# Attention scores: three products of 308 columns, or one of 308 and two of 154

## The chip, the cores and the metric

The kernel runs on one core of a Trainium2 chip. The metric is the time on the device in microseconds (us), the median of the runs shown. The core's engines are TensorE (PE in the profile, its weight loads PEld), VectorE (DVE), ScalarE (ACT), GpSimd (POOL) and SyncE (SP), whose queue issues the DMAs here. Each works through its own queue in order and meets the others at semaphores.

## The reference, cut to what matters

The inputs are x, 32 batches of 512 rows by 640 columns, and a context of 32 batches of 77 rows by 1024. There are 20 heads of 32 columns.

```python
q = _heads(hidden_states @ to_q_w)
h_txt = _sdpa(q, _heads(ehs_txt @ to_k_w), _heads(ehs_txt @ to_v_w))
...
s = jnp.einsum('bhqd,bhkd->bhqk', q, k) * scale
p = jax.nn.softmax(s, axis=-1)
return jnp.einsum('bhqk,bhkd->bhqd', p, v)
...
out = out @ to_out_w + to_out_b
out = (out + residual) / RESCALE
```

The context has exactly 77 rows, so the three further groups of keys (object, others, image) are empty and add nothing. Each head's scores are 512 x 77 numbers, a sum over the head's 32 columns.

## The kernel before, in words

**High and low parts.** All matrix products are of float32r operands. To keep float32 precision each operand is split in two float32r tiles: `split` (L100) lets ScalarE copy the source, which rounds it (the high part, L101), and VectorE subtract that from the source (the low part, L102). A product is then three matmuls into one PSUM tile: high x high, high x low and low x high (`PAIRS`, L120).

**First phase.** Up to about 295 us the kernel turns the context into keys and values, in five groups of 512 or fewer context rows. The keys' high and low parts go out to `k_dram` (L176), the values' to `v_dram`. The weights of the queries and of the output are split as well. This phase's order is made by a scheduler.

**Slots.** Then come 160 slots, each a call of `slot(n)`: batch b = n // 5, chunk j = n % 5 of four heads. From here the order on each engine is as written (`manual_schedule`). A slot has four score tiles t of 128 rows. `scores` (L334) multiplies the 128 queries of the four heads (128 partitions, 32 for each head) with the key tile kb, which is block diagonal: head i's keys stand in partitions 32 i to 32 i + 31 and in columns 77 i to 77 i + 76, and all else is zero. So one matmul of 308 columns gives the scores of four heads. VectorE takes the maximum of each head (nm), `exps` (L353) lets ScalarE write the exponentials and their sums. Three PSUM buffers hold score tiles.

Around that, a slot n works on several n at once:

- `queries(n + 1)` (L316) makes the next chunk's queries in the PSUM tile pq, and `split_q` (L330) splits them into qt, of which there are two.
- `normalize(n - 1)` on GpSimd (L373) divides, and `transpose_p` (L377) transposes on VectorE to z and stores z to DRAM (pd). `load_p` (L393) brings pd back, with keys in the partitions (raw), for a chunk two slots back.
- `cast_p` (L400) and `rest_p` (L407) split raw into pp: ScalarE L404 and L410, VectorE L411, GpSimd L414. The slot begins with `cast_p` on ScalarE.
- `values` (L422) multiplies pp with vb into pa, `split_a` splits that into at.
- `piece` (L472) makes a part of an earlier batch's output, `finish` (L480) adds the residual and bias and stores it.
- The next batch's x is loaded at j = 4 (`load_x`), transposed on VectorE (`transpose_x`, L264) and split (`split_x`, L268) by ScalarE and GpSimd, at the places that `TRANSPOSE_X` and `SPLIT_X` name for each j: three lists, for the three places in a slot. The split x lies in eight buffers xt, five to a batch.
- `refill` (L512) is the slot's first step. At j = 0 and 2 it issues `load_keys` (L295), four DMAs for one of the two groups of chunks; at j = 1 and 3 it issues `load_values`. All go through SP's queue, in order, in front of raw, the residual and pd's stores of that slot.

In the first slots, up to n = 3, no values and no output are made, so TensorE has less to do there.

Of the kernel before, what the change touches and what calls it, by code (L numbers as in the profile page):

```python
# [8 lines left out]
F32 = mybir.dt.float32  # L9
FPR = mybir.dt.float32r  # L10
AF = mybir.ActivationFunctionType
ALU = mybir.AluOpType
# [11 lines left out]
P = 128  # L24
Q = 32
HEADS = 20
HD = 32
# [23 lines left out]
def kernel(  # L51
# [21 lines left out]

    nc = tc.nc
    B, S, C = x.shape
    CA = ehs.shape[2]
# [82 lines left out]
    def keys(g0, gn, j, k):  # L161
        if k == 0:
            pks[j] = psk.tile([P, G], F32, tag="ps", name="pk")
        for n, (a, c) in enumerate(PAIRS):
            nc.tensor.matmul(  # L165
                pks[j][:, :gn],
                wk_s[:, k, a, j * P : (j + 1) * P],
                cts[k][:, c, :gn],
                start=(k == 0 and n == 0),
                stop=(k == NK - 1 and n == 2),  # L170
            )
        if k == NK - 1:
            pk = pks.pop(j)
            ks = kvt.tile([P, 2, G], FPR, tag="ks", name="ks")
            split(ks[:, 0, :gn], ks[:, 1, :gn], pk[:, :gn])
            nc.sync.dma_start(  # L176
                k_dram[:, j, :, g0 : g0 + gn].bitcast(F32), ks[:, :, :gn].bitcast(F32)
            )

    values_of = {}  # L180

# [96 lines left out]

    kbs, vbs, pnb = [], [], []
    for g, (j0, nj) in enumerate(GROUPS):  # L280
        kb = main.tile([P, nj, 2, KCOLS], FPR, name=f"kb{g}")
        nc.gpsimd.memset(kb.bitcast(F32), 0.0)
        kbs.append(kb)
# [4 lines left out]
    qts = [main.tile([P, 2, S], FPR, name=f"qt{n}") for n in range(2)]  # L288
# [5 lines left out]

    def load_keys(b, g):  # L295
        j0, nj = GROUPS[g]
        for i in range(HPC):
            r = slice(i * HD, (i + 1) * HD)
            nc.sync.dma_start(
                kbs[g][r, :, :, i * NKEY : (i + 1) * NKEY].bitcast(F32),  # L300
                k_dram[r, j0 : j0 + nj, :, b * NKEY : (b + 1) * NKEY].bitcast(F32),
            )

    def load_values(b, g):
        j0, nj = GROUPS[g]
# [22 lines left out]
                )  # L328

    def split_q(n):  # L330
        qt = qts[n % 2]
        split(qt[:, 0, :], qt[:, 1, :], pqs.pop(n))

    def scores(n, t):  # L334
        b, j = divmod(n, NC_)
        g = GROUP_OF[j]
        qt, kb = qts[n % 2], kbs[g][:, j - GROUPS[g][0]]
        sc = ps.tile([P, S], F32, tag="sc", name="sc", bufs=3)
        for m, (a, c) in enumerate(PAIRS):
            nc.tensor.matmul(  # L340
                sc[:, :KCOLS],
                qt[:, a, t * P : (t + 1) * P],
                kb[:, c, :],
                start=(m == 0),
                stop=(m == 2),
            )
# [88 lines left out]

    def split_a(n):
        if n >= N - NC_ + 1:
            at = main.tile([P, 2, S], FPR, tag="xt", name="at", bufs=8)
# [72 lines left out]

    def refill(b, j):  # L512

        if j == 0 and b >= 1:
            load_keys(b, 1)
        elif j == 1 and b >= 1:
            load_values(b, 0)
        elif j == 2 and b + 1 < B:
            load_keys(b + 1, 0)
        elif j == 3 and b >= 1:  # L520
            load_values(b, 1)

    def slot(n, beside=None):
# [210 lines left out]
```

## Time and profile before

| | |
|---|---|
| median of 3 runs | 2027.37 us (2027.36 to 2029.03) |
| the profiled execution | 2028.15 us, its span 2026.0 us |
| granted TensorE clock, mean | 0.991 |
| TensorE busy | 1990.2 us of the span (98%) |
| ScalarE busy | 1397.0 us (69%) |
| VectorE busy | 1253.3 us (62%) |
| GpSimd busy | 1051.7 us (52%) |
| DMA, hardware queue | 530013 packets, 414.77 MB, 78.7% of 16 engines' span |
| score matmuls | 1920 of 308 columns, 640 tiles |
| one batch (five slots) in the steady part | 52.95 us |

How to read it: a span is the time from the first to the last instruction of one profiled execution; the run that holds it is a little longer. A group's line gives source line, engine, operation, output<-input, shapes, count, then the busy time in us, the mean of one in ns and the engine's idle time ahead of it with what ended it. A matmul's duration includes the way through the array and overlaps with the next, so what a matmul costs in a row of them is the distance from one start to the next. A bracket behind a line of the timeline is idle time ahead of it and what released it.

### The profile page before, as it was taken

What the parts mean: (1) busy time and instruction counts of PE and PEld (TensorE: products, weight loads), DVE (VectorE), ACT (ScalarE), POOL (GpSimd) and SP (SyncE); (2) the same over time, 40 slices, a digit from 0 to 9 for tenths busy, and PEclk for the clock granted to TensorE, in tenths of its full rate; (3) what the DMA queues carried; (4) which work ended last, traced back from release to release, by engine and by line L of the source; (5) the groups of instructions that cost most, each with busy time, mean ns of one, the idle gap of its engine ahead of it and who ended that gap; (6) DMA issues with size and microseconds to landing.
All of it is one profiled execution on the core that took longest, in us unless ns stands there. A gap on an engine that the chain in (4) does not pass through costs nothing.

```text
span 2026.0 us, 37077 instructions
## 1 busy us (share of the span) xinstructions
PE 1990.2 (98%) x11012; PEld 1802.7 (89%) x11012; DVE 1253.3 (62%) x1999; ACT 1397.0 (69%) x6057; POOL 1051.7 (52%) x615
## 2 busy tenths in 40 slices
PE   8899997999999999999999999999999999999998
PEld 7799986899999999999999999999999999999997
DVE  5443235566666666666666666666666666666663
ACT  3322127777778777777777777777778777787772
POOL 0000024666666666666656566666666666666654
PEclk9999998999999999999999999999999999999999
DMA  7963267988888888888888888888888887888865
GB/s 188 250 217 99 103 151 167 230 211 218 219 219 218 211 220 217 214 215 221 218 216 219 210 223 207 216 216 222 218 215 211 214 216 214 220 215 216 221 187 157
DMA packets 530212, 417.14 MB, mean 206 GB/s; under 512 B 144415, under 2 KB 433725, under 8 KB 530013
## 3 DMA queue, kind: packets, MB, share of 16 engines
q1 hardware_dynamic: 530013, 414.77, 78.7%
q8 instruction: 90, 1.47, 0.3%
q14 instruction: 109, 0.89, 0.1%
HBM read 239.30 MB, written 175.32 MB: 205 GB/s over the span
## 4 chain that ended last, share of the span: by engine, by line
PE 92%; DMA 3%; SPq 1%; ACT 1%; DVE 1%; issue 0%; POOL 0%; DVEq 0%; ACTq 0%; POOLq 0%
PE po L458 28%; PE pq L322 27%; PE pa L428 15%; PE sc L340 13%; PE pk L165 5%; PE pv L191 5%; DMA cs<-in_ctx_dram 1%; ACT pn L358 1%; DMA raw<-pd 0%; SPq L149 0%; SPq L111 0%; DVE z L380 0%; DMA xs<-in_x_dram 0%; DMA wraw<-in_L_xattn_to_out_w_dram 0%; SPq L387 0%
## 5 line engine op out<-in xcount | busy, mean ns | idle before, releaser
L358 ACT ACTIVATE pn<-sc,nm 128x77 f32<-128x77 f32 x2560 | 799.4, 329 | 105.1 <-DVE nm L348 101.4
L458 PE MATMUL po<-wo_s,at 128*128 128x320 f32 x3840 | 615.9, 310 | 5.2 <-DVE xr L486 5.2
L322 PE MATMUL pq<-xt,wq_s 128*128 128x512 f32 x2400 | 610.9, 395 | 0.0
L458 PEld LDWEIGHTS po<-wo_s,at 128*128 128x128 f32 x3840 | 576.5, 188 | 5.8 <-DVE xr L486 5.5
L414 POOL TENSOR_TENSOR pp<-raw,pp 64x512 fp32r<-64x512 f32 x160 | 283.2, 1770 | 512.5 <-ACT pp L410 510.0
L358 ACT ACTIVATION_READ_ACCUMULATOR pn<-sc,nm 128x1 f32 x2560 | 530.3, 207 | 0.0
L322 PEld LDWEIGHTS pq<-xt,wq_s 128*128 128x128 f32 x2400 | 437.3, 188 | 79.8
L348 DVE TENSOR_REDUCE nm<-sc 128x4 f32<-128x308 f32 x640 | 299.7, 469 | 297.0 <-PE sc L340 294.9
L373 POOL TENSOR_TENSOR pn<-pn,rs 128x1232 f32<-128x1232 f32 x160 | 364.1, 2276 | 33.1 <-DVE rs L368 20.9
L340 PE MATMUL sc<-kb,qt 128*128 128x308 f32 x1920 | 377.8, 306 | 2.4 <-ACT qt L101 1.7
L340 PEld LDWEIGHTS sc<-kb,qt 128*128 128x128 f32 x1920 | 325.4, 188 | 45.2 <-ACT qt L101 2.4
L428 PE MATMUL pa<-pp,vb 128*128 128x512 f32 x1280 | 331.5, 401 | 10.7 <-ACT pp L404 9.5
L380 DVE STREAM_TRANSPOSE z<-pn 128x1280 f32<-128x1280 f32 x160 | 241.8, 1511 | 78.8 <-POOL pn L373 29.4
L428 PEld LDWEIGHTS pa<-pp,vb 128*128 128x128 f32 x1280 | 246.0, 198 | 49.9 <-ACT pp L404 10.0
L274 POOL TENSOR_TENSOR xt<-xs,xt 128x512 fp32r<-128x512 f32 x157 | 202.6, 1294 | 149.0 <-ACT xt L273 145.6
L101 ACT CAST at<-pa 128x512 fp32r<-128x512 f32 x160 | 94.0, 588 | 256.8 <-PE pa L428 256.6
L411 DVE TENSOR_TENSOR pp<-raw,pp 128x1024 fp32r<-128x1024 f32 x160 | 196.1, 1226 | 50.6 <-ACT pp L404 50.3
L451 POOL TENSOR_TENSOR xr<-xr,bias 128x640 f32<-128x640 f32 x128 | 201.4, 1574 | 1.8 <-DMA xr<-in_x_dram 1.7
L404 ACT CAST pp<-raw 128x1024 fp32r<-128x1024 f32 x160 | 169.4, 1059 | 5.3 <-DMA raw<-pd 4.9
L165 PE MATMUL pk<-ct,wk_s 128*128 128x512 f32 (+1 forms) x600 | 137.8, 391 | 9.8 <-ACT ct L101 9.8
L191 PE MATMUL pv<-wv_s,ct 128*128 128x320 f32 (+1 forms) x960 | 143.6, 311 | 1.8 <-DVE vs L102 1.8
L191 PEld LDWEIGHTS pv<-wv_s,ct 128*128 128x128 f32 (+1 forms) x960 | 140.9, 186 | 4.0 <-DVE vs L102 2.1
(37 smaller groups left out, 1099.1 us busy)
## 6 DMA issues: line engine op xcount, KB each, us to landing
pd<-z SPq DMA_DIRECT2D x640, 160.0 KB, 3.8
raw<-pd SPq DMA_DIRECT2D x160, 512.0 KB, 4.2
xs<-in_x_dram SPq DMA_DIRECT2D x128, 320.0 KB, 7.5
xr<-in_x_dram SPq DMA_DIRECT2D x128, 320.0 KB, 4.7
out_dram<-xr SPq DMA_DIRECT2D x128, 320.0 KB, 3.5
raw<-pd SPq DMA_DIRECT2D x160, 128.0 KB, 4.4
v_dram<-vs SPq DMA_DIRECT2D x19, 640.0 KB, 3.7
k_dram<-ks SPq DMA_DIRECT2D x20, 512.0 KB, 3.3
```

Of the source, the lines that this page charges most:

```text
L165: nc.tensor.matmul(pks[j][:, :gn], wk_s[:, k, a, j * P : (j + 1) * P], cts[k][:, c, :gn], start=(k == 0 and n == 0), stop=(k == NK - 1 and ...
L191: nc.tensor.matmul(pv[:tn, :HALF], cts[k][:, a, t0 : t0 + tn], wv_s[:, k, c, h * HALF : (h + 1) * HALF], start=(k == 0 and n == 0), stop=( ...
L274: engine.tensor_tensor(parts[1], src, parts[0].bitcast(F32), ALU.subtract)
L322: nc.tensor.matmul(pqs[n], wq_s[:, k, a, j * P : (j + 1) * P], xts[b, k][:, c, :], start=(k == 0 and m == 0), stop=(k == NC_ - 1 and m == 2),)
L340: nc.tensor.matmul(sc[:, :KCOLS], qt[:, a, t * P : (t + 1) * P], kb[:, c, :], start=(m == 0), stop=(m == 2),)
L348: nc.vector.tensor_reduce(nm, sc[:, :KCOLS].rearrange("p (h k) -> p h k", k=NKEY), AX.X, ALU.max, negate=True)
L358: nc.scalar.activation(pnb[n % 2][:, at, :NKEY], sc[:, i * NKEY : (i + 1) * NKEY], AF.Exp, bias=nm[:, i : i + 1], accum_out=sms[n][:, at : ...
L373: nc.gpsimd.tensor_tensor(pf, pf, rs.unsqueeze(2).to_broadcast([P, NQ * HPC, NKEY]), ALU.mult)
L380: nc.vector.transpose(z.rearrange("p b t j -> p t b j"), pn.rearrange("p (t h) k -> p t (h k)", t=NQ).rearrange("p t (b i) -> p t b i", i=Q),)
L414: nc.gpsimd.tensor_tensor(pp[64:, 4, :], raw[:64, 2, :], pp[:64, 4, :].bitcast(F32), ALU.subtract)
L428: nc.tensor.matmul(pas[n], vb[:, t, :, a], pp[:, c, :], start=(m == 0), stop=(m == len(PASSES) - 1),)
L458: nc.tensor.matmul(pos[b, t, h][:, :HALF], ats[b * NC_ + j][:, a, t * P : (t + 1) * P], wos[0][:, j, c, h * HALF : (h + 1) * HALF], start= ...
```

## The change

The score tile's three products become one of 308 columns and two of 154.

- The first is as before: high queries of all four heads with high keys, block diagonal, 308 columns.
- The second makes the columns of heads 0 and 1. These two heads fill only 64 partitions. In the other 64 the new query tile holds a second copy of the same two heads: low queries in partitions 0 to 63, high queries in 64 to 127. The new key tile kc holds the high keys under the low queries, and the low keys under the high queries. So one matmul of 154 columns adds both low x high and high x low.
- The third does the same for heads 2 and 3, with halves exchanged.

To make them, `split_q` writes three query tiles and not two: ScalarE's high copy as before, then for each half one subtraction on VectorE (64 partitions) and one copy on ScalarE of 64 partitions from PSUM into the opposite half. The keys are stored in DRAM in the arrangement that kc needs, by four DMAs of 64 partitions for one before. `load_keys` issues two DMAs for each head, kb (high keys) and kc (both), eight for four before.

The tile qt grows by half, and xt has seven buffers for eight. The transposes and splits of the next x move: the splits are two at j = 2 and three at j = 3, where they were one, two and two at j = 1, 2 and 3. In the middle of the slot `finish` stands before the transposes and not behind. The keys of the second group and the values of batch 0 are loaded in the first slots and no longer ahead of them.

```diff
+            for w in range(2):
+                for half in range(2):
+                    nc.sync.dma_start(
+                        k_dram[half * 64 : half * 64 + 64, j, w, g0 : g0 + gn].bitcast(F32),
+                        ks[w * 64 : w * 64 + 64, int(half != w), :gn].bitcast(F32),
+                    )
...
-        xt = main.tile([P, 2, S], FPR, tag="xt", name="xt", bufs=8)
+        xt = main.tile([P, 2, S], FPR, tag="xt", name="xt", bufs=7)
...
+        kb = main.tile([P, nj, KCOLS], FPR, name=f"kb{g}")
+        kc = main.tile([P, nj, 2, KCOLS // 2], FPR, name=f"kc{g}")
...
     def load_keys(b, g):
         j0, nj = GROUPS[g]
+        kb, kc = kbs[g]
+        src = k_dram[:, j0 : j0 + nj, :, b * NKEY : (b + 1) * NKEY].bitcast(F32)
         for i in range(HPC):
-            r = slice(i * HD, (i + 1) * HD)
+            r, half = slice(i * HD, (i + 1) * HD), i % 2 * NKEY
             nc.sync.dma_start(
-                kbs[g][r, :, :, i * NKEY : (i + 1) * NKEY].bitcast(F32),
-                k_dram[r, j0 : j0 + nj, :, b * NKEY : (b + 1) * NKEY].bitcast(F32),
-            )
+                kb[r, :, i * NKEY : (i + 1) * NKEY].bitcast(F32), src[r, :, i // 2, :]
+            )
+            nc.sync.dma_start(kc[r, :, :, half : half + NKEY].bitcast(F32), src[r])
...
     def split_q(n):
-        qt = qts[n % 2]
-        split(qt[:, 0, :], qt[:, 1, :], pqs.pop(n))
+
+        qt, pq = qts[n % 2], pqs.pop(n)
+        nc.scalar.copy(qt[:, 0, :], pq)
+        lower, upper = slice(0, 64), slice(64, P)
+        for w, (r, other) in enumerate(((lower, upper), (upper, lower))):
+            nc.vector.tensor_tensor(
+                qt[r, 1 + w, :], pq[r], qt[r, 0, :].bitcast(F32), ALU.subtract
+            )
+            nc.scalar.copy(qt[other, 1 + w, :], pq[r])
...
+        for m, (cols, keys_) in enumerate(
+            (
+                (slice(0, KCOLS), kb[:, jg]),
+                (slice(0, half), kc[:, jg, 0]),
+                (slice(half, KCOLS), kc[:, jg, 1]),
+            )
+        ):
             nc.tensor.matmul(
-                sc[:, :KCOLS],
-                qt[:, a, t * P : (t + 1) * P],
-                kb[:, c, :],
+                sc[:, cols],
+                qt[:, m, t * P : (t + 1) * P],
+                keys_,
...
-    TRANSPOSE_X = {0: ((), (0,), (1,)), 1: ((2,), (3,), ())}
-    SPLIT_X = {1: ((), (0,)), 2: ((1,), (2,)), 3: ((3,), (4,))}
+    TRANSPOSE_X = {0: ((), (0,), ()), 1: ((1,), (2,), ()), 2: ((3,), (), ())}
+    SPLIT_X = {2: ((0,), (1,)), 3: ((2, 3), (4,))}
...
-        if j == 0 and b >= 1:
+        if j == 0:
             load_keys(b, 1)
-        elif j == 1 and b >= 1:
+        elif j == 1:
             load_values(b, 0)
...
+        finish()
         for i in turns[1]:
             transpose_x(b + 1, i)
-        finish()
...
         load_keys(0, 0)
-        load_keys(0, 1)
-        for g in range(2):
-            load_values(0, g)
```

More of the change, by code (lines that the diff above doesn't have):

```diff
@@ L175, in keys @@
             split(ks[:, 0, :gn], ks[:, 1, :gn], pk[:, :gn])
-            nc.sync.dma_start(
-                k_dram[:, j, :, g0 : g0 + gn].bitcast(F32), ks[:, :, :gn].bitcast(F32)
-            )
+            for w in range(2):
[4 more added lines that the diff above has]
+                    )
     values_of = {}
@@ L280 @@
     for g, (j0, nj) in enumerate(GROUPS):
-        kb = main.tile([P, nj, 2, KCOLS], FPR, name=f"kb{g}")
-        nc.gpsimd.memset(kb.bitcast(F32), 0.0)
-        kbs.append(kb)
+        kb = main.tile([P, nj, KCOLS], FPR, name=f"kb{g}")
+        kc = main.tile([P, nj, 2, KCOLS // 2], FPR, name=f"kc{g}")
+        for tile_ in (kb, kc):
+            nc.gpsimd.memset(tile_.bitcast(F32), 0.0)
+        kbs.append((kb, kc))
     for n in range(2):
@@ L287 @@
         pnb.append(pn)
-    qts = [main.tile([P, 2, S], FPR, name=f"qt{n}") for n in range(2)]
+    qts = [main.tile([P, 3, S], FPR, name=f"qt{n}") for n in range(2)]
     z = main.tile([P, NBLK, NQ, Q], F32, name="z")
@@ L336, in scores @@
         g = GROUP_OF[j]
-        qt, kb = qts[n % 2], kbs[g][:, j - GROUPS[g][0]]
+        qt, (kb, kc) = qts[n % 2], kbs[g]
+        jg = j - GROUPS[g][0]
         sc = ps.tile([P, S], F32, tag="sc", name="sc", bufs=3)
-        for m, (a, c) in enumerate(PAIRS):
+        half = KCOLS // 2
+        for m, (cols, keys_) in enumerate(
[5 more added lines that the diff above has]
+        ):
             nc.tensor.matmul(
-                sc[:, :KCOLS],
-                qt[:, a, t * P : (t + 1) * P],
-                kb[:, c, :],
+                sc[:, cols],
+                qt[:, m, t * P : (t + 1) * P],
+                keys_,
                 start=(m == 0),
@@ L437, in split_a @@
         if n >= N - NC_ + 1:
-            at = main.tile([P, 2, S], FPR, tag="xt", name="at", bufs=8)
+            at = main.tile([P, 2, S], FPR, tag="xt", name="at", bufs=7)
         else:
@@ L519, in refill @@
             load_keys(b + 1, 0)
-        elif j == 3 and b >= 1:
+        elif j == 3:
             load_values(b, 1)
```

## The prediction

> **What bounds the kernel now.** I read the page's busy times first, then PE's timeline over one slot (a slot is one of the 160 calls of `slot`, one group of four heads in one batch), then the groups and the waits.
>
> ```profile
> PE 1990.2 (98%) x11012; PEld 1802.7 (89%) x11012; DVE 1253.3 (62%) x1999; ACT 1397.0 (69%) x6057; POOL 1051.7 (52%) x615
> ```
>
> TensorE is busy 98% of the span; the next engine, ScalarE, 69%. A busy share may hide gaps, so the slot from 1001.66 (the third of a batch's five, j = 2) follows; columns are start, length with the pipeline's tail, line, count.
>
> ```profile
> 1001.66 0.59 PE L340 MATMUL sc<-kb,qt 128*128 128x308 f32 x3
> 1002.09 1.55 PE L322 MATMUL pq<-xt,wq_s 128*128 128x512 f32 x6
> 1003.48 0.60 PE L340 MATMUL sc<-kb,qt 128*128 128x308 f32 x3
> 1003.91 2.26 PE L322 MATMUL pq<-xt,wq_s 128*128 128x512 f32 x9
> 1006.00 0.60 PE L340 MATMUL sc<-kb,qt 128*128 128x308 f32 x3
> 1006.44 1.92 PE L458 MATMUL po<-wo_s,at 128*128 128x320 f32 x12
> 1008.20 2.04 PE L428 MATMUL pa<-pp,vb 128*128 128x512 f32 x8
> 1010.07 0.59 PE L340 MATMUL sc<-kb,qt 128*128 128x308 f32 x3
> ```
>
> Only starts matter. Three score matmuls take 1002.09 - 1001.66 = 0.43 us, or 0.142 each; 512 columns take (1006.00 - 1003.91)/9 = 0.232, 320 columns 1.76/12 = 0.147. All are near 0.46 ns a column, and no idle time stands in a row: in the steady slots TensorE's streaming sets the time. A slot of 10.59 us is 12 x 0.142 + 15 x 0.232 + 24 x 0.147 + 8 x 0.234 = 10.58. Whatever leaves TensorE's list shortens the kernel, as long as the other engines keep up.
>
> **Part 1, the narrow products.** Each of 640 score tiles had three matmuls of 308 columns. It keeps one and gets two of 154. Streaming alone prices 154 columns at 154 x 0.46 = 0.071 us. But each matmul still loads 128x128 weights (its slice of queries), and that load is no longer covered by 142 ns of streaming. Its price shows where TensorE had been waiting and nothing covers it: two narrow stretches of the weight-load timeline, in the first score tile.
>
> ```profile
> 295.01 0.19 PEld L340 LDWEIGHTS sc<-kb,qt 128*128 128x128 f32 x1 [1.12 <-ACT qt L101]
> ```
>
> ```profile
> 295.11 0.19 PEld L340 LDWEIGHTS sc<-kb,qt 128*128 128x128 f32 x1
> ```
>
> The second load starts 0.10 to 0.11 us after the first (106 ns by the records), not 0.19: a load holds the path for about 0.107 us, and the rest of the 0.19 is latency. In the steady slots a load starts as the matmul before it starts. So a 154-column matmul is followed no sooner than 0.107 us later. Bounds: 0.071 (load fully hidden) and 0.142 (nothing gained); I take 0.108. The Trainium skill, TensorE: Matmul & The Clock Gate, section Back-to-back issue gap, gives N/2.4 + 2.5 ns for an isolated matmul: 67 ns for 154 columns. By that rule a tile saves 2 x (142 - 67) = 150 ns, 96 us in all; by the load row it saves 2 x (142 - 108) = 68 ns, or 640 x 0.068 = **43.5 us**. I take the row: the same rule would put 308 columns at 131 ns, and the trace has 142.
>
> The other end is worse. No fp32r matmul in this trace has fewer than 308 columns. FP8 and Floating Point Precision, TensorE Precision Notes, says that true FP32 takes four passes. The rows at 0.46 ns a column are one pass. Should the narrow form be run in four, each costs 154 x 4 x 0.46 = 0.283 us and the sum is 1280 x (0.283 - 0.142) = 180 us worse. Nothing here shows a dependence on the width, so this stays a rival.
>
> **Part 2, split_q.** Rows for its old pieces and for a copy of 64 partitions:
>
> ```profile
> L101 ACT CAST qt<-pq 128x512 fp32r<-128x512 f32 x160 | 94.6, 592 | 26.0 <-PE pq L322 25.6
> L102 DVE TENSOR_TENSOR qt<-pq,qt 128x512 fp32r<-128x512 f32 x160 | 109.5, 684 | 23.3 <-ACT qt L101 23.0
> L410 ACT CAST pp<-raw 64x512 fp32r<-64x512 f32 x160 | 100.3, 627 | 0.0
> L414 POOL TENSOR_TENSOR pp<-raw,pp 64x512 fp32r<-64x512 f32 x160 | 283.2, 1770 | 512.5 <-ACT pp L410 510.0
> ```
>
> Half the partitions cost as much as all (627 against 592). So ScalarE gets two copies, 1.18 us a slot (190 us in all), and VectorE one more subtraction, 0.68 us. Cover: ScalarE's busy time in five slots of one batch, from the windows view with j = 0 to 4, is 6.80, 8.28, 9.45, 8.75 and 7.86 us of 10.59. The new slot is 10.59 - 4 x 0.068 = 10.32. Adding 1.18 each, and moving the x splits (0.63 of ScalarE each: none is left at j = 1, two at j = 2, three at j = 3) gives 7.98, 8.83, 10.63, 10.56, 9.04. ScalarE overruns at j = 2 and 3 by 0.31 + 0.24 = 0.55 us, and j = 4 takes that back. What would be late is pp: the copies L404 and L410 stand behind the exponentials, then GpSimd's L414, then the values matmuls L428. In this slot L414 ran 1004.50 to 1006.28 and L428 started at 1008.20, so 1.9 us are free. Price on the path: 0. Without cover all of the 1.18 us would show, 189 us. VectorE goes from a mean 7.14 to 7.82 us a slot: 0. GpSimd at j = 3 goes from 8.12 to 9.41: 0. Its last split is read soonest: from L414's start, at worst 3.7 us into j = 3, 1.77 + 2.28 + 1.57 + 3 x 1.29 end 13.2 in, or 2.9 into the next slot; its reader stands 0.36 + 1.39 + 0.36 + 7 x 0.232 = 3.7 into that. Moving `finish` ahead of a transpose, and the seventh xt buffer (the eighth falls away), cost 0, since chunks 2 to 4 reuse buffers whose matmuls precede them in TensorE's order.
>
> **Part 3, the key loads.** They double from 4 to 8 DMAs, at j = 0 and j = 2, on SP's queue ahead of raw's loads, pd's stores and the residual. A batch's keys rise from 4 x (57.8 + 38.5) = 385 KB to 578 (high rows alone, then high and low again). That is little beside some 11 MB that a batch moves at 215 GB/s; the queue is the matter. SP at j = 0 (980.48 to 991.07):
>
> ```profile
> 983.71 3.53 SPq L299 DMA_DIRECT2D kb<-k_dram  x4
> 988.31 0.38 SPq L396 DMA_DIRECT2D raw<-pd  x1
> 988.73 0.48 SPq L397 DMA_DIRECT2D raw<-pd  x1
> ```
>
> Raw is issued at 988.31 and lands a median 4.3 us later, at 992.6; the cast of it is the first thing of ScalarE's next slot (991.07), so it has no slack. Four more issues cost between 4 x 0.43 (their median) = 1.7 and 3.5 us, and the 1.07 us between kb and raw may take up some: 0.7 to 3.5 late, I take 1.8, nearest the median. Behind the late cast in ScalarE are L410 and all exponentials of that slot, behind L411 on VectorE the next maximum and `finish`; L428 on TensorE is first to feel it. There the slack is 1.84 us (median at j = 1, from L414's end to L428's start); with TensorE 0.2 earlier, about 1.6. I book 0.2 us for each of 31 batches, 6 us, with bounds 0 and 31 x 1.9 = 59. At j = 2 raw has 1.8 us more slack: 0.
>
> **Part 4, before the steady slots.** In the key phase 25 stores of keys become 100: 75 issues of about 0.42 us, 31 us of queue under TensorE's work, except at one place where it already waited for context loaded behind them:
>
> ```profile
> 75.33 12.62 PE L165 MATMUL pk<-ct,wk_s 128*128 128x512 f32 x43 [5.78 <-ACT ct L101]
> ```
>
> Between -2 and +7; I take +2, as transfers and not issues were the limit there. In slots 0 to 3, some 8 us each, TensorE is not the bound and split_q's extra 0.7 to 1.2 us sits ahead of the transposes: 4 x 1 = +4 (the matmuls' gain there is lost). The loads moved from ahead of the first slot into slots 0 to 3 find SP idle: 0.
>
> **Sum**, against the profiled execution: span 2026.0 - 43.5 + 6 + 2 + 4 = 1994.5. That execution took 2028.15, 2.15 above its span, and 0.78 above the median shown, 2027.37; so 1994.5 + 2.15 - 0.78 = 1995.9, call it **1996 us**, 1.5% faster.
>
> **Rivals.**
> A, four passes in the narrow form: 2027 + 180 = 2207 us. For it: true FP32's price and that no narrow row exists. Against it: 308, 320 and 512 columns lie on one line through zero.
> B, the other side by one mechanism: raw comes too late at j = 1. Each 0.1 us beyond the 1.6 us of slack costs 3.1 us in all; from 1.6 + (43.5 - 6)/31 = 2.8 us of delay on, the gain is gone. With the 3.5 us bound: 2027 - 43.5 + 59 + 6 = 2049. For it: 0.88 us a key load in this very slot; against it, half that is the median.
> C, the load of weights is hidden too: 0.071 each, saving 91 us; ScalarE would then have 47.1 us of work in five slots of 10.02, 94%, and the same lateness would cost some 15 us more: 1963. Against it: the spacing of loads after a wait.
> D, the narrow matmul saves nothing, because what follows a load waits for more than its 0.107 us: 2027 + 2 + 4 + some 3 of late raw, 2036. Against it: after a wait the next load starts at 0.107, and it starts with the matmul.
>
> **How the numbers follow.** Sum 0.53, own range 1980 to 2012 (0.108 +- 0.008 gives 10 us; late raw 0 to 20). A 0.16. B 0.19, from 2010 to 2050, two thirds of it above 2031. C 0.07. D 0.05. A measurement here can tell about 0.2%, 4 us: faster is 0.53 + 0.07 + 0.05 of B = 0.65, same 0.03, slower 0.32. The range leaves out A and little else: 1962 to 2055.
>
> **What would show it.** Starts of the score trio: 142, 108, 108 ns apart, 0.36 us a tile against 0.43; PE still without idle time in steady slots, a batch at 51.6 us against 52.95; ACT's qt group thrice as long; waits of L404 on raw grown at j = 1, and L428 waiting on L414 or L404 by some tenths. Wrong would be: a 154-column row at 0.28 (A), L428 waiting over 1.4 us a batch (B), a trio of 0.28 us (C).

## The result, and the profile after

| | before | after |
|---|---|---|
| median of the timed runs | 2027.91 us | 2160.24 us (2155.03 to 2164.03) |
| ratio, 95% interval | | 1.065 (1.0624 to 1.0676) |
| span of the profiled execution | 2026.0 us | 2160.9 us |
| mean granted TensorE clock | 0.991 | 0.973 |
| first score matmul | 295.0 us | 299.3 us |
| steady batch of five slots | 52.95 us | 56.92 us |
| mean slot, j = 0, 1, 2, 3, 4 | 10.59, 10.59, 10.60, 10.59, 10.58 | 10.31, 10.62, 10.77, 14.02, 11.20 |

The changed kernel is 6.5% slower; 1996 us had been forecast. (A slot's time here is the distance between its first score matmul and the next slot's, as a mean over the slots 20 to 149.) Of the 134.9 us between the spans, 4.3 came before the first score, 23.6 in the first 20 slots, 103.2 in the slots 20 to 149, and 3.8 behind.

The page of the kernel after, its busy times and the two lines of its chain (the work that ended last, followed back):

```profile
PE 2009.1 (93%) x11012; PEld 1784.9 (83%) x11012; DVE 1364.3 (63%) x2159; ACT 1554.8 (72%) x6377; POOL 1049.0 (49%) x617
...
ACT 37%; PE 22%; DVE 15%; DMA 13%; issue 4%; SPq 2%; POOL 0%; ACTq 0%; DVEq 0%; POOLq 0%
ACT pn L383 21%; DVE qt L346 7%; DMA out_dram<-xr 6%; DMA raw<-pd 5%; PE pq L332 5%; PE po L483 5%; ACT qt L349 4%; DVE z L405 4%; PE pk L168 4%; PE pv L197 4%; ACT pp L429 3%; ACT pp L435 3%; PE pa L453 3%; ACT xt L279 3%; ACT qt L343 2%
```

The chain of the kernel before was TensorE alone:

```profile
PE 92%; DMA 3%; SPq 1%; ACT 1%; DVE 1%; issue 0%; POOL 0%; DVEq 0%; ACTq 0%; POOLq 0%
```

So TensorE alone no longer sets the time. ScalarE is busy only 72%, yet the chain runs through it and through the new lines of `split_q`, L349 (the second copies) and L346 (the subtractions). Their groups, with the idle time of the engine ahead of them in the third column:

```profile
L349 ACT CAST qt<-pq 64x512 fp32r<-64x512 f32 x320 | 185.8, 581 | 242.1 <-DVE qt L346 242.1
L346 DVE TENSOR_TENSOR qt<-pq,qt 64x512 fp32r<-64x512 f32 x320 | 220.3, 689 | 220.1 <-ACT qt L343 116.8
L365 PE MATMUL sc<-kc,qt 128*128 128x154 f32 x1280 | 237.3, 261 | 26.9 <-ACT qt L349 26.7
```

The copies are busy 186 us, as priced (190), but ScalarE sits idle another 242 us ahead of them, 320 times. That is a wait that `before` does not have.

TensorE's timeline of `after`, first where nothing disturbs it (from 998.36 the first, j = 1), then in the slot j = 3 that begins at 1021.00:

```profile
998.36 0.31 PE L365 MATMUL sc<-kb,qt 128*128 128x308 f32 x1
998.50 0.34 PE L365 MATMUL sc<-kc,qt 128*128 128x154 f32 x2
998.68 1.60 PE L332 MATMUL pq<-xt,wq_s 128*128 128x512 f32 x6
1000.12 0.30 PE L365 MATMUL sc<-kb,qt 128*128 128x308 f32 x1
...
1030.40 1.52 PE L483 MATMUL po<-wo_s,at 128*128 128x320 f32 x9
1034.53 1.17 PE L483 MATMUL po<-wo_s,at 128*128 128x320 f32 x3 [2.61 <-DVE xr L511]
1035.50 0.46 PE L365 MATMUL sc<-kb,qt 128*128 128x308 f32 x1
1035.76 0.54 PE L365 MATMUL sc<-kc,qt 128*128 128x154 f32 x2
1036.10 2.85 PE L332 MATMUL pq<-xt,wq_s 128*128 128x512 f32 x6
1038.74 0.46 PE L365 MATMUL sc<-kb,qt 128*128 128x308 f32 x1
```

Two readings. Undisturbed, a trio takes 998.68 - 998.36 = 0.32 us, against 0.43 before, and the six matmuls behind it 1.44 (1.39 before). The change does what it says. But at j = 3 TensorE stands still for 2.61 us until VectorE has done `finish` (L511), and after it the same six matmuls take 1038.74 - 1036.10 = 2.64 us. The windows of that stretch say why (the columns are busy time and instructions of PE, PEld, DVE, ACT and POOL, then the granted clock, the DMA share and GB/s):

```profile
1026.00:1031.00 5.00, 5.00 (x31) 4.69 (x31) 3.15 (x6) 4.36 (x19) 3.73 (x3) 1.00 0.56 114
1036.10:1039.00 2.90, 2.90 (x9) 2.32 (x9) 1.49 (x4) 2.90 (x12) 2.63 (x3) 0.50 0.98 229
```

The granted clock is 0.50 after the gap. By the trace's record of the clock that happened 15 times in the slots 20 to 149, for 54.6 us in all, so half of it, 27.3 us or 1.05 us a batch, is lost (before: not once there). A batch thus adds up: 52.95, less 5 x 0.28 for the narrow products, plus 3.45 us of TensorE idle (2.58 of them ahead of L483 at j = 3), plus 1.05 of clock, is 56.05 of the 56.92; the last 0.9 no view sets apart.

Why `finish` is late shows in the waits (waiting engine and line, what it waited for, us in total, times, longest):

```profile
ACT qt L349 <- DVE qt L346: 242.1, 320, 1.0
DVE qt L346 <- ACT qt L343: 116.8, 152, 3.1
DVE qt L346 <- ACT qt L349: 103.2, 160, 0.6
...
PE po L483 <- DVE xr L511: 82.2, 31, 5.7
...
ACT pp L429 <- DMA raw<-pd: 30.3, 28, 2.5
```

and in one `split_q` on ScalarE, then on VectorE:

```profile
1029.76 0.59 ACT L343 CAST qt<-pq 128x512 fp32r<-128x512 f32 x1
1031.11 0.58 ACT L349 CAST qt<-pq 64x512 fp32r<-64x512 f32 x1 [0.75 <-DVE qt L346]
1032.44 0.58 ACT L349 CAST qt<-pq 64x512 fp32r<-64x512 f32 x1 [0.76 <-DVE qt L346]
1033.05 0.33 ACT L383 ACTIVATE pn<-sc,nm 128x77 f32<-128x77 f32 x1
```

```profile
1030.39 0.68 DVE L346 TENSOR_TENSOR qt<-pq,qt 64x512 fp32r<-64x512 f32 x1 [1.49 <-ACT qt L343]
1031.72 0.69 DVE L346 TENSOR_TENSOR qt<-pq,qt 64x512 fp32r<-64x512 f32 x1 [0.64 <-ACT qt L349]
1032.44 1.51 DVE L405 STREAM_TRANSPOSE z<-pn 128x1280 f32<-128x1280 f32 x1
1033.99 0.89 DVE L511 TENSOR_TENSOR xr<-po,xr 128x320 f32<-128x320 f32 x2
```

The four instructions on pq run strictly in turn: subtract, copy, subtract, copy, each on the engine that the one before is not on. From the end of the high copy (1030.35) ScalarE needs 2.70 us to reach its next exponential, 1.16 of it work; VectorE needs 2.09 us to reach z, and `finish` (L511) stands behind z.

### The profile page after: what moved, and what is told of

Its sections match the earlier page's. It is cut to its first block, busy times and chain, and to the rows that moved or that the text cites. A ratio compares the mean times of both kernels' runs of the same rounds, so it can differ in the third digit from the quotient of the medians.

```text
span 2160.9 us, 38084 instructions
## 1 busy us (share of the span) xinstructions
PE 2009.1 (93%) x11012; PEld 1784.9 (83%) x11012; DVE 1364.3 (63%) x2159; ACT 1554.8 (72%) x6377; POOL 1049.0 (49%) x617
## 3 DMA queue, kind: packets, MB, share of 16 engines
q8 instruction: 90, 1.47, 0.3%
## 4 chain that ended last, share of the span: by engine, by line
ACT 37%; PE 22%; DVE 15%; DMA 13%; issue 4%; SPq 2%; POOL 0%; ACTq 0%; DVEq 0%; POOLq 0%
ACT pn L383 21%; DVE qt L346 7%; DMA out_dram<-xr 6%; DMA raw<-pd 5%; PE pq L332 5%; PE po L483 5%; ACT qt L349 4%; DVE z L405 4%; PE pk L168 4%; PE pv L197 4%; ACT pp L429 3%; ACT pp L435 3%; PE pa L453 3%; ACT xt L279 3%; ACT qt L343 2%
## 5 line engine op out<-in xcount | busy, mean ns | idle before, releaser
L483 PE MATMUL po<-wo_s,at 128*128 128x320 f32 x3840 | 637.9, 314 | 82.2 <-DVE xr L511 82.2
L332 PE MATMUL pq<-xt,wq_s 128*128 128x512 f32 x2400 | 645.9, 411 | 0.7 <-POOL xt L280 0.7
L483 PEld LDWEIGHTS po<-wo_s,at 128*128 128x128 f32 x3840 | 568.1, 189 | 90.7 <-DVE xr L511 90.4
L349 ACT CAST qt<-pq 64x512 fp32r<-64x512 f32 x320 | 185.8, 581 | 242.1 <-DVE qt L346 242.1
L346 DVE TENSOR_TENSOR qt<-pq,qt 64x512 fp32r<-64x512 f32 x320 | 220.3, 689 | 220.1 <-ACT qt L343 116.8
L373 DVE TENSOR_REDUCE nm<-sc 128x4 f32<-128x308 f32 x640 | 285.3, 452 | 49.5 <-PE sc L365 48.3
L365 PEld LDWEIGHTS sc<-kc,qt 128*128 128x128 f32 x1280 | 219.3, 193 | 55.9 <-ACT qt L349 35.9
L365 PE MATMUL sc<-kc,qt 128*128 128x154 f32 x1280 | 237.3, 261 | 26.9 <-ACT qt L349 26.7
L365 PE MATMUL sc<-kb,qt 128*128 128x308 f32 x640 | 201.8, 315 | 3.2 <-ACT pn L383 1.4
L429 ACT CAST pp<-raw 128x1024 fp32r<-128x1024 f32 x160 | 170.7, 1067 | 30.3 <-DMA raw<-pd 30.3
L105 DVE TENSOR_TENSOR at<-pa,at 128x512 fp32r<-128x512 f32 x160 | 109.6, 685 | 73.7 <-ACT at L104 72.6
```

The costliest lines, as they stand in the source:

```text
L332: nc.tensor.matmul(pqs[n], wq_s[:, k, a, j * P : (j + 1) * P], xts[b, k][:, c, :], start=(k == 0 and m == 0), stop=(k == NC_ - 1 and m == 2),)
L346: nc.vector.tensor_tensor(qt[r, 1 + w, :], pq[r], qt[r, 0, :].bitcast(F32), ALU.subtract)
L349: nc.scalar.copy(qt[other, 1 + w, :], pq[r])
L365: nc.tensor.matmul(sc[:, cols], qt[:, m, t * P : (t + 1) * P], keys_, start=(m == 0), stop=(m == 2),)
L373: nc.vector.tensor_reduce(nm, sc[:, :KCOLS].rearrange("p (h k) -> p h k", k=NKEY), AX.X, ALU.max, negate=True)
L429: nc.scalar.copy(pp[:, 0:2, :], raw[:, 0:2, :])
```

## The experiments

All were timed beside the kernel before (its median was 2027.1 to 2029.4 us in the six groups of runs). "Ratio" is to that, with its 95% interval. Three explanations were in play at first: ScalarE and VectorE wait for each other on pq; the eight key loads make raw late; or the moved transposes, splits and `finish`, or the narrow products themselves, do harm.

**Copies first.** The two copies directly behind the high copy, the subtractions after, so that the engines don't alternate:

```diff
+        for w, (r, other) in enumerate(halves):
+            nc.scalar.copy(qt[other, 1 + w, :], pq[r])
         for w, (r, other) in enumerate(halves):
             nc.vector.tensor_tensor(
                 qt[r, 1 + w, :], pq[r], qt[r, 0, :].bitcast(F32), ALU.subtract
             )
-            nc.scalar.copy(qt[other, 1 + w, :], pq[r])
```

> The changed kernel with split_q's two second copies on ScalarE put directly behind the high copy, and the two subtractions on VectorE behind them; the same instructions, none fewer. Theory 1 (the waits between ScalarE and VectorE inside split_q, 242 us in all on ScalarE, push ScalarE past TensorE): those waits go, ScalarE's need per batch falls from 47.1 + 7.5 to 47.1 us, below TensorE's 50.9, and the time falls by about 31 x 5.5 = 170 us to 1975 to 2000. Theory 2 (ScalarE's added work itself, bunched at j = 3 with three x splits, is too much): at most 30 us better, above 2125. Theory 3 (key loads on SP make raw late): no change, 2150 to 2170.

Measured: 2187.11 us, ratio 1.0779 (1.0755 to 1.0802), slower still. The alternation is gone, and ScalarE reaches its next exponential 1.22 us after the high copy, not 2.70. But VectorE now waits for all the copies:

```profile
DVE qt L349 <- ACT qt L347: 296.5, 160, 4.3
```

It reaches z 2.67 us after the high copy, where it was 2.09. So what hurts is less ScalarE's waiting than how long VectorE, with z and `finish` behind it, is held; the first explanation, as it stood in the forecast of this run (ScalarE pushed past TensorE), falls.

**Copies from SBUF.** The second copies read the high part that was just written (the same numbers), not pq:

```diff
-            nc.scalar.copy(qt[other, 1 + w, :], pq[r])
+            nc.scalar.copy(qt[other, 1 + w, :], qt[r, 0, :].bitcast(F32))
```

> The changed kernel with the second copies read from the high tile qt in SBUF and not from PSUM's pq, their place in the order unchanged; a copy of 64 partitions then costs about 0.63 us as the other SBUF copies, not 0.58. Theory 1: neither engine waits for the other after the high copy; 1975 to 2000, and queries are ready about 1 us sooner than with the copies first. Theory 2: above 2125. Theory 3: 2150 to 2170.

Measured: 2096.97 us, 1.0333 (1.0314 to 1.0352). The copies' work is all there (320 of 619 ns each), but of the waits on one another only the first is left:

```profile
DVE qt L346 <- ACT qt L343: 119.5, 151, 3.1
```

z follows 1.47 us after the high copy, the exponentials after 1.32. That moves 63 us, nearly half of the loss, with no less work: this part of the price was the waiting. It is not the only cause, since 1975 to 2000 us had been expected.

**Wide products in the new form.** The second and third matmul get 308 columns of kb again; scores are then not the reference's.

```diff
-                (slice(0, half), kc[:, jg, 0]),
-                (slice(half, KCOLS), kc[:, jg, 1]),
+                (slice(0, KCOLS), kb[:, jg]),
+                (slice(0, KCOLS), kb[:, jg]),
```

> The changed kernel with the second and third score product again 308 columns wide, against the high keys, so that the scores are not the reference's; all loads, copies and waits stay. Theory 1 (ScalarE and VectorE, not TensorE, set the slots at j = 2 to 4): TensorE's 0.1 us a tile more, 66 us in all, is hidden in half of the slots at least; 2170 to 2200. If TensorE still set the time everywhere: 2225. If the narrow form were itself the cost (rival A of the prediction): below 2100.

Measured: 2168.24 us, 1.0688 (1.0671 to 1.0705). The narrow products do no harm; while something else sets the time they bring some 8 us (the two intervals just overlap) and not the 43.5 forecast.

**No copies.** `split_q` as before (one copy, one subtraction), high queries x low keys left out:

```diff
-        for w, (r, other) in enumerate(((lower, upper), (upper, lower))):
-            nc.vector.tensor_tensor(
-                qt[r, 1 + w, :], pq[r], qt[r, 0, :].bitcast(F32), ALU.subtract
-            )
-            nc.scalar.copy(qt[other, 1 + w, :], pq[r])
+        nc.vector.tensor_tensor(qt[:, 1, :], pq, qt[:, 0, :].bitcast(F32), ALU.subtract)
...
-                qt[:, m, t * P : (t + 1) * P],
+                qt[:, min(m, 1), t * P : (t + 1) * P],
```

> The changed kernel with the old split_q: one high copy, one low subtraction of 128 partitions, no second copies; the narrow products take the low tile twice, so the scores are not the reference's. Narrow products, key loads, seven xt buffers and the moved x splits stay. Theory 1 and 2: TensorE is the bound again at 10.18 us a slot, 2027 - 66 + 4 to 15 at the start = 1965 to 1980. Theory 3: still slower than before, above 2050.

Measured: 2085.54 us, 1.0279 (1.0261 to 1.0297). All of `split_q` is worth 75 us, of which the waits are 63; the copies' and the extra subtraction's own work is 11 here. Another 58 us of loss remain without any of it.

**Merged key loads.** The kernel without copies, with keys in one tile kk of four planes, three of them stored next to each other in DRAM, so that one DMA for each head brings both kb's and kc's part: four loads a group as before the change, of 86.6 KB.

```diff
-                kb[r, :, i * NKEY : (i + 1) * NKEY].bitcast(F32), src[r, :, i // 2, :]
+                kk[r, first : first + 3, :, half : half + NKEY].bitcast(F32), src[r]
             )
-            nc.sync.dma_start(kc[r, :, :, half : half + NKEY].bitcast(F32), src[r])
```

> As e4 (narrow products, no second copies, so high queries with low keys are left out of the scores), but the keys of both forms in one tile of four planes and in DRAM in three, so that a group's keys come by four DMAs again, with the bytes of eight. Theory K (the eight key loads on SP's queue delay raw and the stores of pd, and through them TensorE at j = 1 and 3): e4's 4 us a batch above TensorE's 50.9 go, 1960 to 1980. Theory S (the moved x transposes and splits, three at j = 3, the seventh buffer): only the 1.2 us at j = 1 goes, the rest at j = 3 stays: about 2045.

Measured: 2041.54 us, 1.0055 (1.0036 to 1.0074): 44 us less, at the same bytes in the slots, although raw is issued only 0.9 us sooner at j = 0 (10.03 us into the slot for 10.96, medians) and 1.2 us at j = 2. (The first score comes some 10 us later, at 306.4 us; what differs ahead of it is the keys' stores, with one plane stored twice.)

**Before, with eight loads.** The other way round: the kernel before, each key load cut in two, nothing else.

```diff
-            nc.sync.dma_start(
-                kbs[g][r, :, :, i * NKEY : (i + 1) * NKEY].bitcast(F32),
-                k_dram[r, j0 : j0 + nj, :, b * NKEY : (b + 1) * NKEY].bitcast(F32),
-            )
+            for w in range(2):
+                nc.sync.dma_start(
+                    kbs[g][r, :, w, i * NKEY : (i + 1) * NKEY].bitcast(F32),
+                    k_dram[r, j0 : j0 + nj, w, b * NKEY : (b + 1) * NKEY].bitcast(F32),
+                )
```

> The kernel before with each key load cut in two, one for the high and one for the low rows: the same bytes, eight DMAs for four at j = 0 and 2, nothing else. Theory K: raw comes several us later at j = 1, 2040 to 2075. Theory S: 2026 to 2032.

Measured: 2073.99 us, 1.0216 (1.0195 to 1.0238), 46 us slower from four more DMAs of the same bytes, twice a batch. SP's queue in a slot j = 0 of this kernel (start 1002.83):

```profile
1008.40 5.37 SPq L300 DMA_DIRECT2D kb<-k_dram  x8
1013.87 0.38 SPq L397 DMA_DIRECT2D raw<-pd  x1
```

Raw is issued 11.0 us into the slot; in the row of `before` that the forecast quotes it was 988.31 - 980.48 = 7.8. As medians: at j = 0, 10.94 against 7.13; at j = 2, 8.78 against 4.65. Raw then lands 4.51 us (j = 0) and 2.71 us (j = 2) into the next slot; before it was +0.68 and -1.52. Both are late by some 4 us. TensorE, which never waits in the slots 20 to 149 of the kernel before, now waits there 0.57 us a batch ahead of `piece` (L459) for `finish`, and 0.34 us ahead of `values` (L429) for pp.

**Old turns.** The kernel without copies, and the same with merged loads, each with the transposes, splits, `finish` and eight xt as before:

```diff
-    TRANSPOSE_X = {0: ((), (0,), ()), 1: ((1,), (2,), ()), 2: ((3,), (), ())}
-    SPLIT_X = {2: ((0,), (1,)), 3: ((2, 3), (4,))}
+    TRANSPOSE_X = {0: ((), (0,), (1,)), 1: ((2,), (3,), ())}
+    SPLIT_X = {1: ((), (0,)), 2: ((1,), (2,)), 3: ((3,), (4,))}
...
-        finish()
         for i in turns[1]:
             transpose_x(b + 1, i)
+        finish()
```

> As e4 (no second copies, high queries with low keys left out), with eight key loads, but with the x transposes, splits, finish and eight xt buffers of the kernel before. Theory K: as e4 or little better, 2065 to 2090. Theory S: the 1.8 us at j = 3 go, 2030.

> As e4 with both: four merged key loads and the old turns (no second copies, high queries with low keys left out). Both theories: TensorE alone sets the time, five slots of 10.18; 2027 - 66 and 0 to 15 at the start: 1960 to 1980. If it stays above 2000, neither is the cause.

Measured: 2087.60 us, 1.0276 (1.0248 to 1.0305), against 2085.54 without; and 2040.41, 1.0057 (1.0042 to 1.0072), against 2041.54. Without the second copies the moved turns cost nothing; with the copies the old turns were not tried.

That left a puzzle. The second of these kernels has the narrow products, no second copies and four key loads, and it is still not faster than `before`, nor near the forecast. Its slots at j = 0, 2 and 4 take 10.35 to 10.39, but j = 1 takes 10.98 and j = 3 11.10. Its waits show a DMA:

```profile
DVE z L407 <- DMA pd<-z: 120.0, 29, 5.3
```

against, in the kernel before,

```profile
DVE z L380 <- DMA pd<-z: 26.6, 21, 2.2
```

and this is SP's queue, from the slot j = 4 (986.11) into j = 0 (996.47):

```profile
991.42 0.38 SPq L423 DMA_DIRECT2D raw<-pd  x1
991.85 0.47 SPq L424 DMA_DIRECT2D raw<-pd  x1
992.42 2.36 SPq L275 DMA_DIRECT2D xs<-in_x_dram  x4
994.82 1.90 SPq L474 DMA_DIRECT2D xr<-in_x_dram  x1
996.76 3.38 SPq L414 DMA_DIRECT2D pd<-z  x4
1000.25 0.76 SPq L517 DMA_DIRECT2D out_dram<-xr  x1
1001.71 4.57 SPq L316 DMA_DIRECT2D kk<-k_dram  x4
1006.59 0.39 SPq L423 DMA_DIRECT2D raw<-pd  x1
```

The four loads of x (320 KB each) come first, pd's stores behind them, then the keys, then raw, 10.1 us into its slot.

**Keys once.** Is it the keys' larger number of bytes? The last kernel, keys loaded for batch 0 alone (scores of later batches are then not the reference's):

```diff
-        if j == 0:
+        if j == 0 and b == 0:
             load_keys(b, 1)
...
-        elif j == 2 and b + 1 < B:
+        elif j == 2 and b + 1 < 1:
```

> As e7 (narrow products, old turns, no second copies), but the keys are loaded for batch 0 only and all batches use them: no key loads in the steady slots, and the scores of the other batches are wrong. Theory K2 (what is left in e7 is the key loads' own bytes and issues): 1965 to 1980. Theory X (what is left is the next x, four loads of 320 KB issued ahead of pd's stores at j = 4[...], so that z at j = 0 waits for pd): better by part only, 2000 to 2035.

Measured: 2034.54 us, 1.0028 (1.0011 to 1.0045). Six us; the keys are not what is left. From 500 to 1900 us the share of the DMA engines falls from 0.85 to 0.80, and yet z waits for pd as long as with the keys (112.0 us there, 107.7 with them).

**x later.** The load of x behind pd's stores, in three kernels: the merged one with old turns, the full change with SBUF copies and merged loads, and the kernel before.

```diff
-        if j == 4 and b + 2 < B:
-            load_x(b + 2)
...
+        if j == 4 and b + 2 < B:
+            load_x(b + 2)
```

> As e7 (no second copies), with merged key loads, but the next x is loaded behind pd's stores of j = 4 and not ahead of them; the same loads and bytes. Theory X: z at j = 0 no longer waits for pd, TensorE sets the time, 1965 to 1990. Theory K2: 2035 to 2045.

> The changed kernel in full (all three products of high and low), with the second copies read from SBUF, merged key loads and the next x loaded behind pd's stores. Theory 1 with K and X (three causes: the alternation in split_q, eight key loads, x ahead of pd): ScalarE at 47.5 of 50.9 us a batch still fits, 1975 to 2010. If ScalarE's bunched work at j = 2 and 3 is a fourth cause: above 2020.

> The kernel before, with the next x loaded behind pd's stores of j = 4. All theories: TensorE sets the time there already and nothing waits, 2024 to 2030; it says whether e10's and e11's gain is the change's or the load's.

Measured: 2060.23 (1.0165, 1.0146 to 1.0183), 2113.66 (1.0428, 1.0412 to 1.0444) and 2030.73 us (1.0013, 1.0006 to 1.0020). The first is 20 us worse than with x early: raw at j = 0 is issued 2.1 us sooner (8.15 us into the slot for 10.28, medians), but takes 7.65 us to land beside the x transfers (4.66 with x early), and the slot j = 1 takes 11.76 us for 10.98.

**x at j = 0.** The same with the load behind raw of j = 0 (the transposes one slot later, the splits and `finish` placed as in the change):

```diff
-        if j == 4 and b + 2 < B:
-            load_x(b + 2)
+        if j == 0 and b >= 1 and b + 1 < B:
+            load_x(b + 1)
```

> As e7, but the next x is loaded at j = 0, behind raw's load and not at j = 4, with its transposes at j = 1 and 2 and its splits two at j = 2 and three at j = 3. e10 put x behind pd and thereby in front of raw of j = 0, which then took 8 us to land; here it is behind both. Theory X: 1970 to 2000. If a batch is held at 53 us by something other than x: 2035 to 2050.

> The changed kernel in full (nothing left out), with second copies from SBUF, merged key loads and the next x loaded at j = 0 as in e14. Theory X with the alternation and the key loads as causes: 1985 to 2020, faster than the kernel before. If ScalarE's bunched work at j = 2 and 3 costs by itself: 2040 to 2080.

Measured: 2061.83 (1.0182, 1.0160 to 1.0205), and for the full change with SBUF copies and merged loads 2109.65 (1.0411, 1.0393 to 1.0428). In the first, raw of j = 0 now lands in time (0.11 us into the next slot, 4.63 with x at j = 4), but raw of j = 1 is later (4.82 for 3.26), and the slot j = 2 takes 11.44 us.

**A quarter of x.** From the third batch on one of the four loads of x alone (x is then stale, and the output not the reference's). A second kernel has in addition the two narrow products at 308 columns.

```diff
-        for q in range(4):
+        for q in range(4 if b < 2 else 1):
```

> As e7 (narrow products, four merged key loads, old turns, no second copies), but from batch 2 on only one of the four loads of x is made, so the x of those batches is wrong in three quarters of the partitions; all transposes and splits stay. Theory X (the 1.28 MB of x at j = 4 hold up pd's stores, and through them z and raw at j = 0 and the values at j = 1): TensorE sets the time, 51 us a batch, 1965 to 1985. If something else holds a batch at 53 us: 2030 to 2045.

> As e13 (a quarter of x's loads from batch 2 on, merged key loads, no second copies), with the second and third product 308 columns wide again, so that the scores are wrong too. With TensorE alone setting the time in both, the difference to e13's 2001 us is what the narrow products are worth: 640 x (426 - 326 ns) = 64 us, so 2065. By the prediction's 68 ns a tile: 2044.

Measured: 2001.03 us, 0.9869 (0.9855 to 0.9884), and 2034.81, 1.0036 (1.0022 to 1.0049). With less of x to fetch all slots are alike (10.33 to 10.37 us), z no longer waits for pd, and TensorE has no idle time, in the windows of the first as of the second:

```profile
500.00:1900.00 1400.00, 1400.00 (x7985) 1267.23 (x7983) 964.33 (x1542) 1116.22 (x5006) 884.48 (x515) 1.00 0.79 206
```

```profile
500.00:1900.00 1400.00, 1400.00 (x7802) 1269.51 (x7802) 955.58 (x1508) 1093.94 (x4892) 862.65 (x501) 1.00 0.77 201
```

This pair is the clean measurement of the narrow form: 33.8 us, with batches of 51.76 and 52.96 us. One tile of each, narrow and then wide:

```profile
1009.40 0.50 PE L370 MATMUL sc<-kk,qt 128*128 128x308 f32 x3
1009.73 1.59 PE L341 MATMUL pq<-xt,wq_s 128*128 128x512 f32 x6
1011.16 0.48 PE L370 MATMUL sc<-kk,qt 128*128 128x308 f32 x3
```

```profile
1010.10 1.55 PE L341 MATMUL pq<-xt,wq_s 128*128 128x512 f32 x6
1011.49 0.59 PE L370 MATMUL sc<-kk,qt 128*128 128x308 f32 x3
1011.92 0.39 PE L341 MATMUL pq<-xt,wq_s 128*128 128x512 f32 x1
```

From one trio to the next it is 1.76 us here and 0.43 + 1.39 = 1.82 there, 60 ns a tile.

**Four quarters.** Do x's bytes hold the rest up, or the number of its DMAs? Four loads, each of a quarter of the bytes:

```diff
-            nc.sync.dma_start(xs[q * Q : (q + 1) * Q, :, :], src[q])
+            nc.sync.dma_start(xs[q * Q : (q + 1) * Q, :na, :], src[q][:, :na, :])
```

> The kernel with merged key loads and the old turns (2040 us), in which from the third batch on each of the four loads of x moves only a quarter of its bytes: 80 KB each, 320 KB a batch in place of 1280, but still four DMAs. The x of later batches is mostly left stale, so the output is not the reference's. With one load of 320 KB and three left out the same kernel took 2001 us. If the bytes of x hold up what follows in the queue, this kernel takes the same, 2001 +- 5. If the number of DMAs ahead of the stores of pd holds it up, it stays at 2040 +- 5. In between, both count by their distance.

Measured: 2001.44 us, 0.9868 (0.9848 to 0.9888), the same as with one load; raw at j = 0 is issued 3.7 us into its slot here, 3.8 there. It is the bytes.

**The full change with both causes mended.** SBUF copies and merged loads together, nothing left out:

> The changed kernel in full, with the second copies read from SBUF (as e2) and merged key loads (as e5), x loaded at j = 4 as before. If the causes add up: e2's 2097 less the 44 us that merging took from e4, 2053. If ScalarE's second copies add nothing once they don't wait: 2042, as e5.

Measured: 2060.22 us, 1.0162 (1.0145 to 1.0179). The two mends give 100 us of the 132. The second copies with their subtractions still cost 19 us against the merged kernel without them (2041.54), and 2060 is above both figures that had been expected, 2053 and 2042; the slot j = 3 takes 11.87 us for 11.08. Whether that is their work or the three splits at j = 3 beside them, no run sets apart. It is the fastest form of the narrow score tile that was found with all of its computation, and slower than the kernel before.

## Why the prediction was wrong, step by step

**Part 1, the narrow products: the sum nearly right, in part by luck.** 0.108 us for a narrow matmul had been taken, 68 ns a tile, 43.5 us. An undisturbed slot of `after` takes 10.31 us, forecast 10.32. Where TensorE alone sets the time the form is worth 60 ns a tile in the merged form of the key tile, 33.8 us. So 43.5 was some 10 too high: 5 for the 60 ns (640 x 0.060 = 38.4), and the rest mostly in the first ten slots, where it saves nothing (102.0 us wide, 103.1 narrow). The trio was forecast at 142, 108, 108 ns; it is 141, 71, 111. So "followed no sooner than 0.107 us later" is wrong for the matmul itself. It is the weight loads begun beside these matmuls that start 141, 108 and 111 ns apart, and the lead of a load on its matmul shrinks from 139 ns to 68 (medians of the slots 20 to 149). The trio therefore saves 102 ns and not 68, and the matmuls behind it give some 40 of them back (1.44 us for 1.39, without that lead); the two errors nearly cancel. D (nothing saved), C (71 ns each) and A (four passes; the rows of 154 columns show a mean of 261 ns with their tail) fall.

**Part 2, split_q: the step that failed.** "Price on the path: 0" was argued from busy times: ScalarE gets 1.18 us, and each slot has room. That the new copies *wait* was not priced at all. They are ordered with VectorE's subtractions since both read the PSUM tile pq: with qt as their source these waits are gone. The Trainium skill says so, in PSUM — Partial Sum Buffer, section PSUM bank collisions raise a hardware error: two engines, ScalarE and VectorE reading included, must not touch one bank in one group of 32 partitions at the same time, and must be ordered by semaphores. The trace agrees with an order on every one of 320 copies, 242 us of waiting; it is even stricter than the page asks, since the second subtraction, on the other 64 partitions, waits for the first copy too (103 us). The edit removing these waits moved 63 us. All of Part 2 is 75 us where 0 stood for ScalarE and 0 for VectorE, and the 1.9 us that "are free" ahead of L428 did not help, since the first to come late was another: VectorE's z and then `finish`, for which `piece` (L483) waits at j = 3. Time from the high copy's end to z, and the result, in the forms with eight loads: 1.31 us without copies (2085.5), 1.47 from SBUF (2097.0), 2.09 in turn (2160.2), 2.67 copies first (2187.1).

**Part 3, the key loads: mechanism right in part, size wrong.** Raw "0.7 to 3.5 late, I take 1.8" at j = 1, 6 us in all, and "at j = 2 raw has 1.8 us more slack: 0". Measured on the kernel before with nothing else changed: 3.8 us later at j = 0 and 4.1 at j = 2, 46 us. The failing terms are the delay of the issues, taken at 1.8 where the very row showed 3.53 us for four, and the step that set the second group's to nothing; the late raw also cost more in each batch than the 0.2 us booked. And L428 was not "first to feel it": more of TensorE's waiting is ahead of `piece`, for `finish`, which the forecast named behind the late cast and left out of the price. Rival B named this mechanism, and its bound for it, 59 us, holds the 46; with Part 1 alone it would have cancelled the gain.

**Part 4, the start: too small.** +6 was forecast; the first score is 4.3 us later and the first 20 slots cost 23.6 us more. Of these `split_q` is the larger part: the first 20 slots take 215.9 us without the second copies, 223.7 with copies from SBUF and 232.5 in turn (before 208.9), so 7.8 are its work and 8.8 its waits.

**What no step held: the transfers' margin.** The forecast let the narrow products' time go straight into the end, "as long as the other engines keep up", and looked at engines only. Without the second copies and with merged loads the kernel is at 2040, not at 2001. What is missing comes back when x's bytes are cut, in one DMA or in four. That `before` already waited for pd 21 times was to be read in its views. The mean share of the DMA engines does not tell it: it is 0.84 in `before`, 0.80 without key loads at 2034.5 us, and 0.79 with a quarter of x at 2001.0. What counts is the burst ahead of the stores and of raw, and moving it elsewhere only moved the stall. With wide products and a quarter of x a batch takes 52.96 us, as `before` does (52.95), so x's burst does not hold a kernel with wide products; it shows once TensorE needs less. That the kernel before, with its own keys and nothing but shorter score matmuls, would be held likewise was not tried.

**The sum.** 2027.9 - 34 (Part 1) + 75 (Part 2) + 46 (Part 3) + 39 (transfers, 2040 against 2001) is 2154, with 2160 measured; the four were measured apart, on different kernels (the merged ones start 10 us later, `after` loses more in its first slots), and the last two both show as raw landing late, so their sum is no proof. Both larger terms were among the forecast's parts, priced 0 and 6.

## What to carry to other kernels

When an edit lets a second engine read a PSUM tile that another is reading, price the chain of the alternating reads and what stands behind it on both engines, not the busy time; read from SBUF what is there already. Count DMAs ahead of an urgent one at their full price in that very row, at each place where they are issued. Before crediting an engine's gain to the end, take it away from the transfers' margin too: look for bursts that stand in the queue ahead of urgent stores and loads, and for waits on these in the list, not at the mean busy share alone.

## What the hardware showed that was not expected

- Gaps of TensorE that average 82.2 / 31 = 2.65 us (the waits of L483) were followed, about every second time, by a stretch of 3.41 or 6.83 us at a granted clock of 0.50. All stretches at 0.50 in this trace begin on one grid of 3.413 us. In the slots 20 to 149 TensorE was busy for at most 0.38 of each of the 15 windows of that grid that a stretch follows, and for at least 0.47 of each of the 403 other windows at full clock. So what counts is how a gap lies on the grid. The gap that ends at 977.09 is cut in two by it, in the first two rows, and no stretch follows; the one that ends at 1034.53 lies for the most part in the window of the third row, and the stretch begins at 1034.05:

```profile
972.61:976.02 3.41, 1.87 (x13) 1.57 (x11) 2.40 (x3) 1.87 (x6) 3.07 (x2) 1.00 0.87 241
976.02:979.44 3.42, 2.35 (x13) 2.09 (x14) 2.45 (x5) 3.42 (x15) 1.92 (x2) 1.00 0.75 172
1030.64:1034.05 3.41, 1.29 (x9) 1.02 (x7) 2.70 (x4) 2.16 (x9) 2.48 (x2) 1.00 0.85 226
```

  The Trainium skill, TensorE: Matmul & The Clock Gate, The HAM clock gate, names that window, 3413 ns and running free, and the stretches after these gaps are one or two of it; but it asks for an idle window of about 3.4 us, and here windows that were idle for 62% sufficed.
- In a trio of 308, 154 and 154 columns, the starts are 141, 71 and 111 ns apart, those of the weight loads 141, 108 and 111: the first narrow matmul uses up the lead of the loads, and the second is followed at their pace.
- Cutting four key loads (57.8 or 38.5 KB each) in two, at the same bytes, made raw, issued behind them, 4 us later, 1 us for each DMA added; four loads of x with a quarter of the bytes each cost no more than one whole load (2001.44 and 2001.03 us, raw issued at the same place in its slot).
